# Channel statistics of an output projection: bn_stats on VectorE, or sums on ScalarE

## The chip, the cores and the metric

The kernel runs on one NeuronCore of one Trainium2 chip, in fp32 throughout. The metric is the device time of one execution in microseconds, the median of several runs. The engines are named as in the profile: PE (TensorE matmul; PEld is its weight load), DVE (VectorE), ACT (ScalarE), POOL (GpSimd), SP (SyncE, which issues nearly all DMAs).

## The reference, cut to what matters

Layer 0 is a Mamba-like block on x of shape (4, 128, 128, 128): batch B=4, C=128 channels, L=128*128=16384 positions, 256 inner channels, 16 states. Layer 1 is a group norm, a small softmax over four filters, and a product of 2D Fourier transforms.

```python
h1 = relu(xf @ mlp_w1.T + b1);  xm = h1 @ mlp_w2.T + b2
x_in, z = split(xm @ in_proj_w.T)
u = silu(causal_conv4(x_in) + conv_b)            # 256 channels
dt, Bm, Cm = split(u @ x_proj_w.T);  delta = softplus(dt @ dt_proj_w.T + dt_b)
h = h * exp(delta*A) + delta*u*Bm;  y = sum_s h*Cm   # a scan over L, 256 x 16 rows
y = (y + u*D) * silu(z)
out = y @ out_proj_w.T                            # C=128: the output projection
g = group_norm(out, 4 groups)                     # mean and variance over (C/4, H, W)
x1 = silu(g * gn_w + gn_b) + x
# layer 1: group norm of x1 (32 groups over x1 twice), 1x1 conv, relu, mean over (H, W),
# softmax over 4 filters; irfft2(sum_f w_f * X * FF_f) + residual_weight * x1
```

What the change touches is how the mean and variance of `out`, which the 4-group norm needs, are gathered.

## The kernel before, in words

`block0` (layer 0) cuts each batch into 32 chunks of T=512 positions, 128 chunks in all, and runs them as a software pipeline whose order is written out by hand: every piece of work is a Python function entered in `todo[slot, phase]`; a chunk has 16 slots (`NP`), and within a slot the phases run in the order turn, sums, pe, exps, late, act, pool, dbu, gate, scans, dve, end (L492 to L497). Each engine executes its own instructions in this order. Buffers come from pools, whose reuse adds waits.

**The scan.** A pair of slots is one unit of four scans (128 rows by 512 positions). `exps(n)` (L376) makes exp(delta*A) on ACT into four tiles `da0` to `da3`, of which three are single PSUM buffers; it stands one slot ahead of its use. `scans(n)` (L389) runs the recurrence on DVE (L405). In an even slot its two results go to a tile `h`, which POOL multiplies by C (L412). In an odd slot DVE multiplies them itself (L407), and ACT copies the last column out for the next chunk (L408, `st<-da`). `by_vector` (L338) decides which engine takes which h*C product. `dbu` (L344) makes delta*u*B on POOL (L354), and `sums` (L415) adds the states on PE (L426).

**The work beside it**, by its slot in the chunk: slot 2, `silu_act` (L227) for the chunk to come and `z_silu` (L232) on ACT, and `gate(1)` (L436) on DVE; slot 4, `o_mm` (L438), the output projection, and `xd_act` (L242); slot 5, `o_act` (L443), which copies the projection out of PSUM and sends it to a DRAM tile, and `dt_mm` (L255); slot 6, `dt_act` (L262), the softplus. Silu and softplus are in other activation tables than exp, so each brings an ACT_TABLE_LOAD before it and one before the next exp. `o_stats` (L451), the `bn_stats` of the projection, stands in slot 2 of the chunk after that one. (`o_mm` and `o_act` of a chunk lie in the slots of the next chunk, so that its statistics come two chunks late.)

The tag `pp` has two PSUM banks that are used in turn: convolution 0, convolution 1, (in some chunks two norm tiles), projection `po`, `dt` 0, `dt` 1. So `dt` 1 takes the bank that `po` leaves.

**Norming chunks.** While batch b+1 is scanned, batch b is finished (`finish`, L541): `group_norm` (L500) turns its statistics into mean and 1/std around slots 7 to 10 of one chunk; then in 16 chunks (`norming`, L329) two tiles each are normalised: `norm_act` (L563, Silu on ACT in slot 2), `norm_dve` (L568) and `norm_stats` (L573) on DVE in slot 3. There are 48 such chunks, and 80 plain ones, where DVE has no such work in slot 3. In the next 16 chunks `agg_act` (L598) runs Relu with an accumulator output on ACT. The last batch is finished inside `block1`, the Fourier part.

`which` is 0 for the 4-group norm of the projection and 1 for the norm of layer 1.

Of the kernel before, what the change touches and what calls it, by code (L numbers as in the profile page):

```python
# [26 lines left out]
F32 = mybir.dt.float32  # L27
AF = mybir.ActivationFunctionType
ALU = mybir.AluOpType
AX = mybir.AxisListType  # L30
# [3 lines left out]
P = 128  # L34
# [112 lines left out]
def block0(tc, s):  # L147
    nc, B, NCH, NH, NS, NG, ND, R, NX, KC, HALO, C, L, NF, DI = (
        s.nc, s.B, s.NCH, s.NH, s.NS, s.NG, s.ND, s.R, s.NX, s.KC, s.HALO, s.C, s.L, s.NF, s.DI,
    )  # L150
    NT = T // P
    with ExitStack() as ctx:
# [13 lines left out]
        def psum(n):  # L166
            return psp.tile([P, T], F32, tag="pp", name=f"pp_{n}")
# [5 lines left out]
        stats, outs = s.stats, s.outs  # L173
# [256 lines left out]
        def post(k):  # L430

            b, i = divmod(k, NCH)
            d = st[k]

            def gate(j):
                nc.vector.tensor_mul(d["zs"][:, j, :], d["zs"][:, j, :], d["y", j])  # L436

            def o_mm():  # L438
                d["po"] = psum(f"o_{k}")
                for j in range(NH):  # L440
                    nc.tensor.matmul(d["po"], s.wo[:, j, :], d["zs"][:, j, :], start=j == 0, stop=j == NH - 1)

            def o_act():  # L443
                if i == 0:
                    stats[b] = s.spool.tile([P, NCH, 6], F32, tag="stats", name=f"stats_{b}")
                    outs[b] = s.opool.tile([C, L], F32, tag="ob", name=f"ob_{b}")
                d["o"] = p2.tile([P, T], F32, tag="o", name=f"o_{k}", bufs=3)
                nc.scalar.copy(d["o"], d["po"])
                nc.sync.dma_start(out=outs[b][:, i * T : (i + 1) * T], in_=d["o"])

            def o_stats():  # L451
                nc.vector.bn_stats(stats[b][:, i, :], d["o"])
                st.pop(k - 1, None)

            return [
                (26, "dve", partial(gate, 0)), (34, "dve", partial(gate, 1)), (36, "pe", o_mm), (37, "act", o_act),
                (50, "dve", o_stats),
            ]

        n_chunks = B * NCH  # L460
# [1 line left out]
        for k in range(n_chunks):  # L462
            for at, phase, f in pre(k) + post(k):
                todo[at + (k - 1) * NP, phase].append(f)
# [35 lines left out]
def group_norm(s, io, b, mat, which, stat, at, then):  # L500


    nc = s.nc
    g = {}

    def small(n, m=1):
        g[n] = io.small.tile([P, m], F32, tag=n, name=f"{n}_{which}_{b}")
        return g[n]

    def aggregate():  # L510
        nc.vector.bn_aggr(small("mv", 2), stat().rearrange("p n q -> p (n q)"))

    def mean_mm():
        ps = g["ps"] = io.psum(f"gm_{which}_{b}")
        nc.tensor.matmul(ps[:, 0:1], getattr(s, mat), g["mv"][:, 0:1], start=True, stop=True)

    def spread_act():
        mv = g["mv"]
        nc.scalar.copy(small("mean"), g["ps"][:, 0:1])
        q = small("q")  # L520
        nc.scalar.activation(q, mv[:, 0:1], AF.Square, scale=-1.0, bias=g["mean"])
        nc.scalar.activation(q, q, AF.Identity, bias=mv[:, 1:2])

    def var_mm():
        ps = g["ps"] = io.psum(f"gv_{which}_{b}")
        nc.tensor.matmul(ps[:, 0:1], getattr(s, mat), g["q"], start=True, stop=True)

    def root_act():
        nc.scalar.activation(small("rstd"), g["ps"][:, 0:1], AF.Sqrt, bias=s.eps)

    def invert():
        nc.vector.reciprocal(g["rstd"], g["rstd"])
        then(g["mean"], g["rstd"])

    return [
        (at, "dve", aggregate), (at, "end", mean_mm), (at + 1, "act", spread_act), (at + 3, "pe", var_mm),
        (at + 3, "act", root_act), (at + 3, "dve", invert),
    ]
# [437 lines left out]
```

## Time and profile before

| | us |
|---|---|
| median of 3 runs (7328.43 to 7332.73) | 7330.66 |
| the profiled execution's own time | 7341.55 |
| its span | 7339.5 |
| block 0: last projection copy starts | 6525.7 |
| busy DVE / POOL / ACT / PE | 7022.4 / 6896.1 / 6064.9 / 5890.0 |
| `bn_stats` of the projection: 128 x 672 ns on DVE | 86.0 |
| its copy out of PSUM: 128 x 577 ns on ACT | 73.9 |

All durations come from the one profiled execution, whose time is 10.89 us (0.15%) above the median. A duration in the profile is longer than the distance to the next instruction's start on the same engine: neighbours overlap by some 0.09 us, so what an instruction takes from its engine is read from starts in the timeline.

### The profile page before, as it was taken

To read this page: it belongs to the slowest core of one execution; us is meant where nothing else is said; L and a number is where in the kernel's file an instruction comes from. 1 tells how busy PE (TensorE), PEld (TensorE's weight loads), DVE (VectorE), ACT (ScalarE), POOL (GpSimd) and SP (SyncE) were. 2 spreads that over 40 slices of the span, in tenths; PEclk is the share of its full clock that TensorE was granted. 3 is DMA by queue.
4 is the path that set the end of the run, shared out by engine and by line. 5 is a ranking of instruction groups with operands and counts; after the bars stand their busy time and mean duration, and the time that the engine had idled before them with its cause. 6 is when DMAs were issued, how large, how long until landed. Compare 5 with 4: busy or idle time off the path is not lost.

```text
span 7339.5 us, 90375 instructions
## 1 busy us (share of the span) xinstructions
PE 5890.0 (80%) x25908; PEld 2648.4 (36%) x25908; DVE 7022.4 (96%) x8168; ACT 6064.9 (83%) x13183; POOL 6896.1 (94%) x3188
## 2 busy tenths in 40 slices
PE   7877877877777788887777788887777788868999
PEld 2322322332222233332222233332222233348999
DVE  7999999999999999999999999999999999978777
ACT  6888888888888888888888888888888888867886
POOL 6999999999999999999999999999999999977787
PEclk8888888888888889898899888888999888889999
DMA  5766666666777767667777676677777766758666
GB/s 139 163 156 148 157 156 155 150 159 165 187 181 176 182 159 166 169 163 178 180 177 188 165 172 167 158 171 173 178 187 173 178 165 156 175 142 255 187 165 169
DMA packets 864134, 1246.32 MB, mean 170 GB/s; under 512 B 78856, under 2 KB 318608, under 8 KB 863632
## 3 DMA queue, kind: packets, MB, share of 16 engines
q1 hardware_dynamic: 863488, 1240.28, 69.2%
q8 instruction: 204, 3.34, 0.2%
q14 instruction: 298, 2.44, 0.1%
q10 hardware_dynamic: 144, 0.26, 0.0%
HBM read 996.97 MB, written 243.27 MB: 169 GB/s over the span
## 4 chain that ended last, share of the span: by engine, by line
DVE 16%; ACT 14%; DMA 14%; PE 12%; issue 5%; POOL 2%; SPq 1%; DVEq 0%; ACTq 0%; POOLq 0%
DVE da L405 7%; ACT da L387 6%; DVE h L405 4%; DMA rdelta<-dd 3%; DMA xt<-in_x 3%; DVE hb L407 2%; PE pp_h L190 2%; DMA of<-ob 2%; ACT bt L295 1%; DMA dd<-delta 1%; DMA rB<-bc 1%; PE pa L780 1%; DMA xr<-in_x 1%; ACT L387 1%; PE y L426 1%
## 5 line engine op out<-in xcount | busy, mean ns | idle before, releaser
L354 POOL TENSOR_TENSOR hb<-rdu,rB 128x1536 f32<-128x1536 f32 (+2 forms) x1536 | 3603.3, 2362 | 38.6 <-DMA rdu<-dd 35.3
L387 ACT ACTIVATE da<-rdelta,amat 128x512 f32<-128x512 f32 x4096 | 2677.1, 694 | 63.2 <-DVE h L405 60.0
L412 POOL TENSOR_TENSOR hb<-h,rC 128x1024 f32<-128x1024 f32 (+1 forms) x1072 | 2433.5, 2272 | 179.2 <-DVE h L405 162.5
L405 DVE TENSOR_TENSOR_SCAN da<-da,st,hb 128x512 f32<-128x512 f32 x1976 | 2425.0, 1272 | 11.7 <-POOL hb L354 5.3
L426 PE MATMUL y<-hb,sel 128*32 128x512 f32 x8192 | 1313.3, 717 | 3.1 <-POOL hb L412 2.7
L407 DVE TENSOR_TENSOR hb<-da,rC 128x512 f32<-128x512 f32 x2040 | 1301.3, 679 | 3.0
L405 DVE TENSOR_TENSOR_SCAN h<-da,st,b 128x512 f32<-128x512 f32 x992 | 1264.1, 1274 | 23.6 <-ACT da L387 7.0
L405 DVE TENSOR_TENSOR_SCAN h<-da,st,hb 128x512 f32<-128x512 f32 x1000 | 1256.8, 1261 | 2.0 <-ACT da L387 1.6
L374 PE MATMUL b<-ident,bt 128*128 128x128 f32 x4096 | 759.9, 309 | 613.3 <-DVE h L405 499.0
L225 PE MATMUL pp_cv<-xm,wck 128*128 128x512 f32 x2048 | 1018.7, 642 | 32.9 <-ACT zs L219 32.0
L374 PEld LDWEIGHTS b<-ident,bt 128*128 128x128 f32 x4096 | 548.7, 157 | 1187.2 <-DVE h L405 788.2
L295 ACT ACTIVATE bt<-pt_dut,xdt 128x256 f32<-128x256 f32 x2048 | 838.2, 471 | 132.4 <-PE pt_dut L284 132.3
L408 ACT COPY st<-da 128x1 f32<-128x1 f32 x2040 | 282.5, 161 | 767.9 <-DVE hb L407 765.8
L225 PEld LDWEIGHTS pp_cv<-xm,wck 128*128 128x128 f32 x2048 | 399.3, 206 | 700.2 <-issue 461.9
L190 PE MATMUL pp_h<-xt,w 128*128 128x512 f32 x512 | 387.3, 899 | 262.5 <-DMA xt<-in_x 208.3
L759 POOL TENSOR_TENSOR wb<-wb,term 128x1040 f32<-128x1040 f32 x192 | 461.0, 2401 | 90.0 <-ACT term L753 75.3
L284 PE MATMUL pt_dut<-ident,du 128*128 128x128 f32 x1024 | 209.3, 326 | 279.8 <-ACT st L408 270.3
L422 PE MATMUL y<-u,diag 128*128 128x512 f32 x512 | 297.8, 665 | 146.8 <-DVE zs L436 146.5
L303 POOL TENSOR_TENSOR du<-delta,u 128x512 f32<-128x512 f32 x256 | 319.1, 1268 | 27.2 <-ACT delta L266 27.2
L387 ACT ACT_TABLE_LOAD x262 | 336.1, 1283 | 4.7
L284 PEld LDWEIGHTS pt_dut<-ident,du 128*128 128x128 f32 x1024 | 126.9, 156 | 574.4 <-POOL du L303 436.2
L190 PEld LDWEIGHTS pp_h<-xt,w 128*128 128x128 f32 x512 | 124.6, 269 | 547.2 <-DMA xt<-in_x 261.1
(138 smaller groups left out, 8084.0 us busy)
## 6 DMA issues: line engine op xcount, KB each, us to landing
rdelta<-dd SPq DMA_DIRECT2D x1024, 256.0 KB, 4.8
rdu<-dd SPq DMA_DIRECT2D x1024, 256.0 KB, 7.8
rC<-bc SPq DMA_DIRECT2D x512, 256.0 KB, 7.5
rB<-bc SPq DMA_DIRECT2D x512, 192.0 KB, 4.8
dd<-delta SPq DMA_DIRECT2D x256, 256.0 KB, 7.3
dd<-du SPq DMA_DIRECT2D x256, 256.0 KB, 6.4
ft<-in_filt_w SPq DMA_DIRECT2D x104, 520.0 KB, 7.0
ob<-o SPq DMA_DIRECT2D x128, 256.0 KB, 2.1
```

The lines of the kernel that those rows point to most:

```text
L190: nc.tensor.matmul(ps["h", j], s.w1[:, j * P : (j + 1) * P], d["xt"], start=True, stop=True)
L225: nc.tensor.matmul(ps["cv", j], w, d["xm"][:, t : t + T], start=t == 0, stop=t == KC - 1)
L284: nc.tensor.transpose(ps["dut"][:, 2 * t + j, :], d["du"][:, j, at : at + P], s.ident)
L295: nc.scalar.activation(d["bt"][:, 2 * h + t, :, q, :], src, AF.Copy, scale=d["xdt"][:, 2 * h + t, R + q : R + q + 1])
L354: nc.gpsimd.tensor_tensor(hb[:, p : p + n, :], d["du", j][:, m : m + n, :], d["B"][:, p - 1 : p - 1 + n, :], ALU.mult)
L374: nc.tensor.transpose(b[:, t * P : (t + 1) * P], src, s.ident)
L387: nc.scalar.activation(d["da", p][q], d["delta", j][:, m, :], AF.Exp, scale=s.amat[:, c : c + 1])
L405: nc.vector.tensor_tensor_scan(o, das[q], b, init, ALU.mult, ALU.add)
L407: nc.vector.tensor_tensor(hb[:, p + q, :], das[q], d["C"][:, p + q, :], ALU.mult)
L412: nc.gpsimd.tensor_tensor(hb[:, ps, :], h[:, q, :], d["C"][:, ps, :], ALU.mult)
L426: nc.tensor.matmul(y[m * DG : (m + 1) * DG, :], s.sel, d["hb", j, r][:, p, :], start=False, stop=r == NG - 1)
L759: nc.gpsimd.tensor_tensor(wb, wb, u[n].terms[f], ALU.add)
```

## The change

The copy of the projection out of PSUM becomes an Identity activation with an accumulator output (the sum per channel), and a second activation, Square in place in PSUM with an accumulator output (the sum of squares), follows it. The `bn_stats` per chunk on DVE is gone; its place in the list only drops a dictionary entry. The statistics tile holds two rows of 32 sums per batch instead of 32 records of six. For this norm `bn_aggr` becomes a `reduce_sum`, and four small ACT instructions turn the sums into mean and variance ahead of the matmul that averages over the group. Which h*C products DVE and POOL take is as before, and so are all DMAs.

```diff
             def o_act():
                 if i == 0:
-                    stats[b] = s.spool.tile([P, NCH, 6], F32, tag="stats", name=f"stats_{b}")
+                    stats[b] = s.spool.tile([P, 2, NCH], F32, tag="stats", name=f"stats_{b}")
                     outs[b] = s.opool.tile([C, L], F32, tag="ob", name=f"ob_{b}")
                 d["o"] = p2.tile([P, T], F32, tag="o", name=f"o_{k}", bufs=3)
-                nc.scalar.copy(d["o"], d["po"])
+
+                nc.scalar.activation(d["o"], d["po"], AF.Identity, accum_out=stats[b][:, 0, i : i + 1])
+                nc.scalar.activation(d["po"], d["po"], AF.Square, accum_out=stats[b][:, 1, i : i + 1])
                 nc.sync.dma_start(out=outs[b][:, i * T : (i + 1) * T], in_=d["o"])
 
-            def o_stats():
-                nc.vector.bn_stats(stats[b][:, i, :], d["o"])
+            def done():
                 st.pop(k - 1, None)
 
             return [
...
-                (50, "dve", o_stats),
+                (50, "dve", done),
             ]
...
     def aggregate():
-        nc.vector.bn_aggr(small("mv", 2), stat().rearrange("p n q -> p (n q)"))
+        mv = small("mv", 2)
+        if which:
+            nc.vector.bn_aggr(mv, stat().rearrange("p n q -> p (n q)"))
+        else:
+            nc.vector.reduce_sum(mv, stat(), axis=AX.X)
 
     def mean_mm():
+        if which == 0:
+            mv, q = g["mv"], small("q")
+            nc.scalar.activation(q, mv[:, 0:1], AF.Square, scale=1.0 / s.L)
+            nc.scalar.mul(q, q, -1.0)
+            nc.scalar.mul(mv[:, 0:1], mv[:, 0:1], 1.0 / s.L)
+            nc.scalar.activation(mv[:, 1:2], mv[:, 1:2], AF.Identity, scale=1.0 / s.L, bias=q)
         ps = g["ps"] = io.psum(f"gm_{which}_{b}")
         nc.tensor.matmul(ps[:, 0:1], getattr(s, mat), g["mv"][:, 0:1], start=True, stop=True)
```

## The prediction

> **What bounds the kernel now.** The first row of the page gives two engines above 90% over the span.
>
> ```profile
> PE 5890.0 (80%) x25908; PEld 2648.4 (36%) x25908; DVE 7022.4 (96%) x8168; ACT 6064.9 (83%) x13183; POOL 6896.1 (94%) x3188
> ```
>
> In block 0 (the first 6560 us) the windows of 500 us show DVE at 489 to 498 us busy and POOL at 479 to 490. So DVE looks like the bound, and the edit takes work from it. The groups by form give that work, and the rows nearest to what is added (the copy that goes, L448, has 577 ns):
>
> ```profile
> L452 DVE BATCH_NORM_STATS2 stats<-o 128x6 f32<-128x512 f32 x128 | 86.0, 672 | 0.0
> L208 ACT ACTIVATE xm<-pp_xm,mlp_b 128x512 f32<-128x512 f32 x128 | 88.0, 687 | 3.5 <-PE pp_xm L200 3.5
> L600 ACT ACTIVATE pp_agg<-pp_agg,bv 128x512 f32<-128x512 f32 x84 | 54.0, 643 | 0.0
> L600 ACT ACTIVATION_READ_ACCUMULATOR pp_agg<-pp_agg,bv 128x1 f32 x84 | 16.1, 192 | 0.0
> ```
>
> A share of 99% doesn't say that DVE is what ends each wait. The timeline of a plain chunk does; first ACT, from slot 1's end to slot 6 (start, duration, both in us):
>
> ```profile
> 1310.81 0.16 ACT L408 COPY st<-da 128x1 f32<-128x1 f32 x1 [0.43 <-DVE hb L407]
> 1310.87 1.31 ACT L387 ACTIVATE da<-rdelta,amat 128x512 f32<-128x512 f32 x2
> 1312.19 1.28 ACT L233 ACT_TABLE_LOAD   x1
> 1313.49 1.06 ACT L233 ACTIVATE zs<-zs 128x1024 f32<-128x1024 f32 x1
> 1314.45 1.25 ACT L230 ACTIVATE u<-pp_cv,conv_b 128x512 f32<-128x512 f32 x2
> 1315.72 1.28 ACT L387 ACT_TABLE_LOAD   x1
> 1317.01 1.30 ACT L387 ACTIVATE da<-rdelta,amat 128x512 f32<-128x512 f32 x2
> ...
> 1321.55 0.58 ACT L448 COPY o<-pp_o 128x512 f32<-128x512 f32 x1
> 1323.20 0.16 ACT L408 COPY st<-da 128x1 f32<-128x1 f32 x1 [1.07 <-DVE hb L407]
> 1323.80 0.16 ACT L408 COPY st<-da 128x1 f32<-128x1 f32 x1 [0.43 <-DVE hb L407]
> ```
>
> and DVE over the same slots 2 to 4:
>
> ```profile
> 1313.06 0.67 DVE L452 BATCH_NORM_STATS2 stats<-o 128x6 f32<-128x512 f32 x1
> 1313.64 0.67 DVE L436 TENSOR_TENSOR zs<-zs,y 128x512 f32<-128x512 f32 x1
> ...
> 1317.78 1.27 DVE L405 TENSOR_TENSOR_SCAN h<-da,st,b 128x512 f32<-128x512 f32 x1
> ```
>
> ACT waits for DVE's last product of slot 1 (1310.81), then works without a gap through exps, a table load, three Silus, a second table load, and delivers the first exp for slot 4 at 1317.01 + 0.69 = 1317.70. DVE starts slot 4's scan at 1317.78, 0.044 us behind the modelled end of that exp. Where DVE does sit waiting for this exp (the first plain chunk of batches 1 to 3, where its scans are a little shorter), it starts 0.033 us behind it. So in slots 2 to 4 of a plain chunk **ACT and DVE are tied within 0.01 us**. Read at the same two places of the timeline, all plain chunks but those of the first batch's ramp show 0.03 to 0.05.
>
> The norming chunk is different. There DVE has four more instructions in slot 3, ACT only two more Silus (first ACT, then DVE):
>
> ```profile
> 1818.46 1.30 ACT L387 ACTIVATE da<-rdelta,amat 128x512 f32<-128x512 f32 x2
> ```
> ```profile
> 1817.86 1.28 DVE L570 TENSOR_TENSOR of<-pp_n,xr 128x512 f32<-128x512 f32 x2
> 1819.05 1.28 DVE L574 BATCH_NORM_STATS2 stats<-of 128x6 f32<-128x512 f32 x2
> 1820.24 1.27 DVE L405 TENSOR_TENSOR_SCAN h<-da,st,b 128x512 f32<-128x512 f32 x1
> ```
>
> The exp is ready at about 1819.15, DVE comes at 1820.24: 1.06 us behind, the same (1.05 to 1.06) in all 48 norming chunks. Here DVE alone is the bound.
>
> **What the Trainium skill says.** "ScalarE: Activation LUTs", section "What ACT_TABLE_LOAD costs", gives about 1283 ns for a load and 186 ns + 0.833 ns per element for an ACTIVATE with immediates, some 93 ns for each pointer operand, and neighbours that overlap by some 93 ns. The trace agrees: every load 1283, the copy 577 (613 by the page), Identity with a pointer bias 687 (706). "ScalarE activation tables: per-element evaluation and per-set limits", section "What a function is on this engine", says that two functions of one set need no load between them and that the accumulator output works with every table. In the trace neither Identity (L208) nor Square (L798, L799) has a load of its own, and the changed program's instruction list has 530 loads, as many as the program before. "SBUF — State Buffer", section "Who interferes with whom", says that a DVE instruction with at most one SBUF input outside the 2-port modes doesn't contend with GpSimd; if so, taking `bn_stats` away does not speed POOL up. No row before isolates that, and I count nothing for it.
>
> **The change part by part.**
>
> *bn_stats removed.* From start to start it takes 1313.64 − 1313.06 = 0.58, 0.586 on average; 128 of them are 75.0 us of DVE. In the 48 norming chunks it all counts: 1.06 − 0.586 leaves 0.47 of lead. POOL follows: its idle time in such a chunk is 1.05 us (0.89 of it before L412 in slot 4, waiting for DVE's h), so 0.47 remains there too. Gain 48 × 0.586 = **28.1 us**. In the 80 plain chunks the exp holds slot 4 where it is: gain 80 × 0.011 = 0.9 at most. What is late next there is ACT, by its two table loads, and DVE will stand 0.57 us before L405 in each.
>
> *o_act longer.* In the Relu rows with an accumulator output the read starts 0.57 us after the activation, and the next instruction 0.09 after the read (2902.53 to 2902.62). Identity to SBUF takes 0.58 to its successor (L208). The block is then 0.58 + 0.09 + 0.57 + 0.09 = 1.33 in place of 0.48: **0.85 us more**, 109 us of ACT in all. It lies in slot 5, where ACT waits 1.07 us for DVE's product and then 0.43 for the second one; only an excess over about 1.6 would delay the exps of slot 6. In a norming chunk the first wait is 1.65, less the 0.586 that DVE is earlier. Cost 0. If the cover went, each us would cost up to 128 us. Behind it stand the softplus and its two loads, after which DVE already waits 0.15 us in slot 8 of every chunk. The bounds: no overlap at all between the four instructions makes 0.69 + 0.19 + 0.66 + 0.19 = 1.73, an excess of 1.25, still 0; below nothing it can't go, since the copy waited for nobody.
>
> *The bank.* `dt` 1 waits for `po`'s bank until Square ends, about 1322.7 to 1323.0 instead of 1322.13. Its matmuls then end near 1324.0; the softplus reads at 1326.47 and PE's next work waits for DVE until 1325.0. Cost 0. SP's send of `o` starts 0.1 to 0.3 us later, and behind it stand loads of rB and rC, which wait for the landing of bc anyway. Cost 0.
>
> *Statistics.* Per batch, `bn_aggr` (1.01) becomes a sum (0.18 by L604). Four ACT instructions (0.23 to 0.33 apart by L521, L522 and L622, together 1.1 us) go in front of slot 8's exps, behind DVE's sum. ACT recovers 0.4 to 0.6 of it in its waits for DVE in slots 9 and 10; the rest delays the Sqrt for which DVE's reciprocal (L532) already waits 2.3 to 2.6 us. With the shorter sum: +0.3 (0 to 1.1) for each of 3 batches, **+0.9**. The last batch's matmul stands on the path in block 1: 0.85 less on DVE against 1.3 more on ACT, **+0.5**. At the end of block 0 the copy is followed by the softmax and then by block 1's first loads (last ACT instruction ends at 6527.35, first load at 6527.38): **+0.85**.
>
> Sum: −28.1 − 0.9 + 0.9 + 0.5 + 0.85 = **−26.8 us**. Against the profiled execution (7341.55, span 7339.5) that is 7314.8; the median of the runs stands 10.89 lower, so 7330.66 − 26.8 = **7303.9**.
>
> **The rivals.**
>
> A. *DVE is the bound everywhere*, and the whole 75.0 us counts, as the shares suggest: 7330.66 − 75.0 + 2.3 = 7258. Against it: the tie in all plain chunks. For it: only that the exps could move if ACT's chain began earlier, which no part of the edit does.
>
> B. *Nothing or a part is gained*, since POOL or a transfer holds the norming chunks. POOL's idle 1.05 us speaks against it; if half of it were needed for its own waits, the gain would be 48 × 0.3 = 14 us, 7319; with none, 7333.
>
> C. *Slower*: ACT's block in slot 5 outgrows its cover, and the exps of slots 6 and 7 and the softplus come late. It decides from an excess of 1.6 us; at 2.1 us, with accumulator reads that drain the engine, it costs 128 × 0.5 = 64, so 7330.66 + 64 − 27 = 7368. Against it: the Relu rows show no such drain.
>
> D. *It doesn't do what it says*: a load of another table around each Square would cost 128 × (2 × 1.28 + 0.85 − 1.6) = 232 us. The count of loads excludes it.
>
> **How the numbers follow.** A measurement can tell about 0.2% from no change, 14.7 us. Main case 0.78 (7296 to 7312), A 0.05, B 0.11, C 0.06, D nil. Main and A are faster by over 0.2%, with a little of B: 0.83; B gives within 0.2%: 0.1; C slower: 0.07. The range takes in the main case, the best part of B and a gain a little past the main case: 7290 to 7321.
>
> **What would show it.** Right: 128 bn_stats gone; plain chunks of the same length (49.2 and 49.95 us in turn between the `xd` copies) with 0.57 us of idle DVE before L405 in slot 4, released by ACT's exp; norming chunks at 50.55 instead of 51.13; POOL's wait in slot 4 of those down from 0.9 to 0.3; Identity and Square with two reads 1.33 us apart from start to next. Wrong: plain chunks that shrink (A), a wait of the slot 6 or slot 8 scans for exps that grows above 0.15 (C), or norming chunks that stay at 51.1 (B).

## The result and the profile after

| | before | after |
|---|---|---|
| median, us (8 runs each) | 7338.79 (7328.43 to 7344.72) | 7315.54 (7304.67 to 7319.75) |
| the profiled execution | 7341.55 | 7313.21 |
| ratio of the times, 95% interval | | 0.9969 (0.9961 to 0.9978) |

The changed kernel is faster by 22.8 us by the ratio (16 to 29 by its interval); between the two profiled executions it is 28.3, against the forecast 26.8. With more runs the median before came out 8 us higher than the three runs that the forecast was set against, so its 7303.9 is best read as a ratio, 0.9964. In absolute terms the median of 7315.54 is 11.6 above the forecast; 8.1 of these are the higher median before.

The first row of the page after. DVE has lost 72.9 us of busy time and ACT has gained 83.8:

```profile
PE 5969.1 (82%) x25908; PEld 2667.5 (36%) x25908; DVE 6949.5 (95%) x8040; ACT 6148.7 (84%) x13583; POOL 6895.5 (94%) x3188
```

The groups by form of the new block (count, busy us, mean ns, idle time before). Each of the two activations has a row of its own for the read of its accumulator, and none has a table load:

```profile
L449 ACT ACTIVATE o<-pp_o 128x512 f32<-128x512 f32 x128 | 75.3, 588 | 2.5 <-PE pp_o L441 2.5
L450 ACT ACTIVATE pp_o<-pp_o 128x512 f32<-128x512 f32 x128 | 74.3, 581 | 0.0
L449 ACT ACTIVATION_READ_ACCUMULATOR o<-pp_o 128x1 f32 x128 | 24.6, 192 | 0.0
L450 ACT ACTIVATION_READ_ACCUMULATOR pp_o<-pp_o 128x1 f32 x128 | 24.0, 187 | 0.0
```

The timeline of the same plain chunk as before, ACT from the end of slot 1 to slot 6 (start, duration, both in us):

```profile
1306.97 0.16 ACT L408 COPY st<-da 128x1 f32<-128x1 f32 x1 [0.43 <-DVE hb L407]
...
1308.35 1.28 ACT L233 ACT_TABLE_LOAD   x1
1309.64 1.06 ACT L233 ACTIVATE zs<-zs 128x1024 f32<-128x1024 f32 x1
1310.60 1.25 ACT L230 ACTIVATE u<-pp_cv,conv_b 128x512 f32<-128x512 f32 x2
1311.87 1.28 ACT L387 ACT_TABLE_LOAD   x1
1313.16 1.30 ACT L387 ACTIVATE da<-rdelta,amat 128x512 f32<-128x512 f32 x2
...
1317.70 0.59 ACT L449 ACTIVATE o<-pp_o 128x512 f32<-128x512 f32 x1
1318.19 0.19 ACT L449 ACTIVATION_READ_ACCUMULATOR o<-pp_o 128x1 f32 x1
1318.28 0.58 ACT L450 ACTIVATE pp_o<-pp_o 128x512 f32<-128x512 f32 x1
1318.80 0.19 ACT L450 ACTIVATION_READ_ACCUMULATOR pp_o<-pp_o 128x1 f32 x1
1319.35 0.16 ACT L408 COPY st<-da 128x1 f32<-128x1 f32 x1 [0.36 <-DVE hb L407]
```

and DVE in slots 2 to 4:

```profile
1309.22 0.65 DVE L436 TENSOR_TENSOR zs<-zs,y 128x512 f32<-128x512 f32 x1
1309.80 2.45 DVE L405 TENSOR_TENSOR_SCAN da<-da,st,hb 128x512 f32<-128x512 f32 x2
1312.17 1.26 DVE L407 TENSOR_TENSOR hb<-da,rC 128x512 f32<-128x512 f32 x2
1313.92 1.28 DVE L405 TENSOR_TENSOR_SCAN h<-da,st,b 128x512 f32<-128x512 f32 x1 [0.49 <-ACT da L387]
```

From the last copy of slot 1 (1306.97) to the first exp for slot 4 (1313.16) ACT needs 6.19 us; before it needed 6.20. The scan of slot 4 starts 0.033 us behind the end of that exp (the median of all plain chunks), which is the distance that the prediction took for a scan that waits. What was `bn_stats` is now a wait. Two products and their overlap would bring DVE to that scan at 1312.17 + 1.19 = 1313.36; it starts at 1313.92, 0.56 later (the bracket shows 0.49, since neighbours usually overlap). The table of waits says the same for the whole run (total us, times, longest): first before, then after. The longest, some 40 us, is the wait at the start of the kernel; without it 25 waits of 11.5 us together have become 98 of 51.6.

```profile
DVE h L405 <- ACT da L387: 52.8, 26, 41.3
```
```profile
DVE h L405 <- ACT da L387: 91.7, 99, 40.1
```

In a norming chunk after (ACT, then DVE, then POOL) the first exp ends at 1815.87 + 0.69 = 1816.56 and DVE arrives at 1817.07, without a wait and 0.51 behind it where it had been 1.09. POOL still waits 0.30 us for DVE in slot 4, where it had waited 0.89; its line before stands last:

```profile
1815.87 1.30 ACT L387 ACTIVATE da<-rdelta,amat 128x512 f32<-128x512 f32 x2
```
```profile
1814.68 1.28 DVE L581 TENSOR_TENSOR of<-pp_n,xr 128x512 f32<-128x512 f32 x2
1815.87 1.27 DVE L585 BATCH_NORM_STATS2 stats<-of 128x6 f32<-128x512 f32 x2
1817.07 1.26 DVE L405 TENSOR_TENSOR_SCAN h<-da,st,b 128x512 f32<-128x512 f32 x1
```
```profile
1819.58 2.35 POOL L412 TENSOR_TENSOR hb<-h,rC 128x1024 f32<-128x1024 f32 x1 [0.30 <-DVE h L405]
```
```profile
1822.77 2.34 POOL L412 TENSOR_TENSOR hb<-h,rC 128x1024 f32<-128x1024 f32 x1 [0.89 <-DVE h L405]
```

**Chunk lengths.** The distance between the `xd` copies of successive chunks, read from the timeline, makes a budget of block 0. It runs from slot 4 of one chunk to slot 4 of the next. A plain length is called even or odd by the first of the two, and a norming length holds the norming work of slot 3 of the second. The table gives, for the before kernel, the changed one and each experiment, the median length of even plain, odd plain and norming chunks, away from the ends of a batch (35, 33 and 45 of them), and "irregular": by how much the sum of these 113 lengths exceeds what it would be with each at the median of its kind.

| kernel | even plain | odd plain | norming | irregular, us | ratio to before (95%) |
|---|---|---|---|---|---|
| before | 49.21 | 49.95 | 51.13 | 17.7 | 1 |
| after | 49.19 | 49.94 | 50.53 | 21.2 | 0.9969 (0.9961 to 0.9978) |
| e1_plain_only | 49.20 | 49.95 | 51.13 | 24.6 | 0.9999 (0.9991 to 1.0007) |
| e2_norming_only | 49.21 | 49.95 | 50.54 | 27.4 | 0.9968 (0.9955 to 0.9981) |
| e3_sums_beside | 49.21 | 49.95 | 51.13 | 21.0 | 1.0003 (0.9995 to 1.0011) |
| e5_before_no_zsilu | 49.20 | 49.95 | 51.13 | 12.6 | 0.9981 (0.9974 to 0.9987) |
| e4_after_no_zsilu | 48.69 | 49.45 | 50.54 | 15.6 | 0.9918 (0.9904 to 0.9931) |
| e7_before_moved | 49.39 | 49.77 | 51.13 | 15.3 | 0.9993 (0.9984 to 1.0001) |
| e6_after_moved | 49.25 | 49.32 | 50.54 | 28.1 | 0.9948 (0.9936 to 0.9961) |
| e8_after_moved_even | 48.92 | 49.36 | 50.54 | 19.1 | 0.9929 (0.9917 to 0.9942) |
| e11_before_load | 49.20 | 49.95 | 51.13 | 3.7 | 0.9972 (0.9962 to 0.9982) |
| e12_before_no_zsilu_load | 49.20 | 49.95 | 51.13 | 1.6 | 0.9964 (0.995 to 0.9978) |
| e9_after_load | 49.20 | 49.94 | 50.54 | 3.7 | 0.9934 (0.9921 to 0.9946) |
| e10_even_load | 48.91 | 49.36 | 50.54 | 2.1 | 0.9876 (0.9863 to 0.989) |

Between the two profiled executions: 45 norming chunks gain 45 × 0.60 = 27.0, and 5.8 comes back as more irregularity in them; plain chunks gain 3.5, of which 2.3 is irregularity; the 12 chunks around the batch ends gain 4.3 (three of these are norming: 1.8); the start gains 1.9; and what follows the last chunk takes 2.7 more. That is 28.

### The profile page after: what moved, and what is told of

Its sections match the earlier page's. It is cut to its first block, busy times and chain, and to the rows that moved or that the text cites. A ratio compares the mean times of both kernels' runs of the same rounds, so it can differ in the third digit from the quotient of the medians.

```text
span 7311.3 us, 90639 instructions
## 1 busy us (share of the span) xinstructions
PE 5969.1 (82%) x25908; PEld 2667.5 (36%) x25908; DVE 6949.5 (95%) x8040; ACT 6148.7 (84%) x13583; POOL 6895.5 (94%) x3188
## 4 chain that ended last, share of the span: by engine, by line
DMA 16%; ACT 16%; DVE 12%; PE 12%; issue 5%; POOL 2%; SPq 1%; DVEq 0%; ACTq 0%; POOLq 0%
ACT da L387 6%; DVE da L405 6%; DMA xt<-in_x 3%; DMA rdelta<-dd 3%; DVE h L405 3%; DMA dd<-delta 2%; DVE hb L407 2%; DMA rB<-bc 2%; DMA of<-ob 2%; PE pp_h L190 2%; ACT L387 1%; DMA xr<-in_x 1%; ACT bt L295 1%; PE y L426 1%; PE pa L791 1%
## 5 line engine op out<-in xcount | busy, mean ns | idle before, releaser
L426 PE MATMUL y<-hb,sel 128*32 128x512 f32 x8192 | 1331.8, 726 | 4.8 <-POOL hb L412 2.9
L258 PE MATMUL pp_dt<-xd,wdt 8*128 8x512 f32 x512 | 290.1, 649 | 80.1 <-ACT pp_o L450 79.2
```

The source lines that it names most:

```text
L426: nc.tensor.matmul(y[m * DG : (m + 1) * DG, :], s.sel, d["hb", j, r][:, p, :], start=False, stop=r == NG - 1)
```

## The experiments

The theory: in plain chunks ACT's chain of table loads and Silus sets slot 4, tied with DVE, so `bn_stats` counts in norming chunks alone; the longer ACT block lies in a wait. The rivals: A, DVE is the bound in every chunk; B, POOL holds the norming chunks; C, ACT's block outgrows its cover.

### bn_stats left out in one kind of chunk only: e1 and e2

Both are the kernel before with a condition in front of `bn_stats`, and the statistics tile filled once per batch.

```diff
# e1_plain_only
-                nc.vector.bn_stats(stats[b][:, i, :], d["o"])
+                if norming(k + 2):
+                    nc.vector.bn_stats(stats[b][:, i, :], d["o"])
# e2_norming_only
-                nc.vector.bn_stats(stats[b][:, i, :], d["o"])
+                if not norming(k + 2):
+                    nc.vector.bn_stats(stats[b][:, i, :], d["o"])
```

> The kernel before, with bn_stats left out in the 80 chunks where its place is a plain chunk, and kept in the 48 norming ones (the statistics are then partly a constant). Tie theory (ACT's two table loads hold slot 4 of a plain chunk): 0 to -2 us; plain chunks stay 49.2 and 49.95 us long and DVE stands 0.49 us idle before L405 in slot 4. Rival A (DVE is the bound everywhere): 80 x 0.586 = -47 us, plain chunks 48.6 and 49.4.

> The mirror: bn_stats left out only where its place is a norming chunk (48), kept in the 80 plain ones. Tie theory: the whole gain, 48 x 0.586 = -28 us, norming chunks 50.54 instead of 51.13. Rival B (POOL holds the norming chunks): -14 us or less. Rival A gives -28 here too, so that this run tells A from the tie only beside its mirror.

Measured beside 7345.09 us for the kernel before: e1 7344.95 (ratio 0.9999, 0.9991 to 1.0007), e2 7318.99 (0.9968, 0.9955 to 0.9981). Eighty `bn_stats` off the busiest engine gained nothing that can be told from zero; the other 48 gained 23.5 us by the ratio, as much as the whole change (22.8). DVE's timeline in e1 shows where the time of a plain chunk goes:

```profile
1313.18 1.27 DVE L407 TENSOR_TENSOR hb<-da,rC 128x512 f32<-128x512 f32 x2
1314.95 1.28 DVE L405 TENSOR_TENSOR_SCAN h<-da,st,b 128x512 f32<-128x512 f32 x1 [0.50 <-ACT da L387]
```

The same wait as in the changed kernel, with nothing changed on ACT: so it is ACT's old chain, tied with DVE, that holds the plain chunks, and not the new ACT work. A falls, and B falls by e2's 50.54.

### The ACT block alone: e3

```diff
-                nc.scalar.copy(d["o"], d["po"])
+                nc.scalar.activation(d["o"], d["po"], AF.Identity, accum_out=sums2[b][:, 0, i : i + 1])
+                nc.scalar.activation(d["po"], d["po"], AF.Square, accum_out=sums2[b][:, 1, i : i + 1])
```

> The kernel before, bn_stats kept and used, with the copy made into Identity and Square with sums that nobody reads (a second small tile): the added ACT work alone, 0.72 us a chunk by the profile after. Tie theory: it lies in ACT's wait of slot 5, 0 to +2 us (only the end of block 0). Rival C (ACT's length counts): up to 128 x 0.72 = +92 us, with exps of slots 6 to 8 late.

Measured: 7345.49 us, 1.0003 (0.9995 to 1.0011). ACT's timeline, at the end of the block:

```profile
1318.82 0.58 ACT L451 ACTIVATE pp_o<-pp_o 128x512 f32<-128x512 f32 x1
1319.34 0.19 ACT L451 ACTIVATION_READ_ACCUMULATOR pp_o<-pp_o 128x1 f32 x1
1319.90 0.16 ACT L409 COPY st<-da 128x1 f32<-128x1 f32 x1 [0.37 <-DVE hb L408]
```

ACT still waits 0.37 us for DVE's product after the block, where it waited 1.07 before it was lengthened. The difference, 0.70, is the block's growth, and all of it comes out of the wait. C falls.

### ACT's chain shortened: e5 and e4

If ACT's chain ties with DVE, shortening it must do nothing for the kernel before and open the wait in the changed one. The Silu of z (1.06 us) is left out.

```diff
-                (NP - 3, "pe", z_mm), (NP - 1, "act", z_act), (NP + 2, "act", z_silu), (3, "pe", xd_mm), ...
+                (NP - 3, "pe", z_mm), (NP - 1, "act", z_act), (3, "pe", xd_mm), ...
```

> The kernel before with z_silu left out (z goes into the gate without its Silu): ACT's work between the two table loads of slot 2 is 0.96 us shorter, with bn_stats still on DVE. Tie theory: DVE alone then holds slot 4, plain chunks stay at 49.2 and 49.95, 0 to -4 us. If ACT rather than DVE were what holds these chunks: up to 80 x 0.57 = -46 us.

> The changed kernel with z_silu left out (z goes into the gate without its Silu): ACT's chain of slot 2 is 0.96 us shorter than the 0.57 us that bn_stats had. Tie theory: the gap before L405 in slot 4 closes and the 80 plain chunks gain what they did not: 80 x 0.57 = -46 us on the changed kernel, -69 us on the kernel before (ratio about 0.9906), plain chunks 48.6 and 49.35. Rivals (POOL or transfers hold the plain chunks): it stays at -23 us.

Measured: e5 (from before) 7329.87, 0.9981 (0.9974 to 0.9987), 14 us faster than before; e4 (from the changed kernel) 7275.73, 0.9918 (0.9904 to 0.9931), 60 us faster than the kernel before (69 expected) and so some 37 faster than the changed one (46 expected). In e4 slot 4 begins without a wait in an undisturbed plain chunk:

```profile
1313.83 1.27 DVE L407 TENSOR_TENSOR hb<-da,rC 128x512 f32<-128x512 f32 x2
1315.01 1.27 DVE L405 TENSOR_TENSOR_SCAN h<-da,st,b 128x512 f32<-128x512 f32 x1
```

The commonest lengths in e4's timeline are 48.61 us for even and 49.36 for odd plain chunks, 0.58 less than in the changed kernel and as expected: `bn_stats` is worth its full 0.586 in a plain chunk once ACT gets out of the way. The medians of the table, 48.69 and 49.45, lie higher because only a third of e4's plain lengths are undisturbed. Counted from 48.61 and 49.36 the irregular part of e4's plain lengths is 18 us, where the changed kernel has 14. By the profiled spans e4 gains 40 us on the changed kernel.

In e5 the plain chunks kept their 49.20 and 49.95, as the tie says. But the 14 us were a miss: more than the 0 to 4 expected, and not in any regular chunk. Of the 7.8 us between the two profiled spans, 5.1 are irregular length and 5.2 lie around the batch ends, with 2.5 lost elsewhere. So the irregular chunks had to be looked at, which led to the last group.

### DVE's work moved ahead of the wait: e7, e6, e8

The new idle time in slot 4 can be used if h\*C work that DVE does behind it is moved ahead of it. In an odd plain chunk DVE takes one extra product in slot 12; here it takes the one in slot 2. In e8 even plain chunks also swap: DVE takes the product in slot 2 and gives one of slot 13 to POOL.

```diff
# e7_before_moved (on before) and e6_after_moved (on after)
-            return p > 1 or (k % 2 == 1 and (j, r, p) == (1, 2, 1))
+            return p > 1 or (k % 2 == 1 and (j, r, p) == (0, 1, 1))
# e8_after_moved_even (on after)
-            return p > 1 or (k % 2 == 1 and (j, r, p) == (1, 2, 1))
+            if k % 2 == 0:
+                return (p > 1 and (j, r, p) != (1, 2, 2)) or (j, r, p) == (0, 1, 1)
+            return p > 1 or (j, r, p) == (0, 1, 1)
```

> The same one-line move in the kernel before, where slot 2 still has bn_stats and no hole. Tie theory: DVE's work is the same and only stands elsewhere, so 0 (-4 to +4 us). If the move were good in itself: about -24 us.

> The changed kernel with one line more: in odd plain chunks DVE takes its extra h*C product in slot 2 (unit 1) instead of slot 12 (unit 6); shares unchanged, all results kept. Tie theory: the product fills the hole of slot 2, odd plain chunks go from 49.94 to about 49.3: 40 x 0.6 = -24 us on the changed kernel (-18 to -30), about -47 us on the kernel before. If DVE's total held the chunks: 0 on the changed kernel. If ACT's chain grows by the copy out of slot 2 (0.08 to 0.16): up to 6 us less gain.

> As the move above, and in even plain chunks too: DVE takes a product in slot 2 and gives one of slot 13 (unit 6) to POOL, results kept. Tie theory: even plain chunks from 49.19 to about 48.7, where POOL's 48.5 us of work comes into sight: -20 us beyond the move alone, about -44 us on the changed kernel. If POOL binds as soon as it is touched: no gain beyond the move, or a few us lost.

Measured beside 7339.49 for before: e7 7334.52, 0.9993 (0.9984 to 1.0001); e6 7296.93, 0.9948 (0.9936 to 0.9961); e8 7288.96, 0.9929 (0.9917 to 0.9942). The same edit shifts 0.18 us from odd to even chunks in the kernel before, with no effect clear of the noise. In the changed one it takes 0.62 off the odd length and adds only 0.06 to the even one: the product leaves an odd length, and slot 2 of an odd chunk lies in the even length before it, at whose end DVE had waited. The idle time was real, and only the changed kernel has it.

Yet by the ratios e6 gains some 15 us on the changed kernel and e8 some 29, by the profiled spans 17 and 42, where 24 and 44 were expected. For e6 the table shows why: its odd chunks fell as expected, but its irregular part is 7 us larger than in the changed kernel. Even chunks in e8 fell to 48.92, not 48.7. In e8's odd lengths POOL waits for nobody any more; in its even ones POOL waits 1.6 us for DVE and DVE stands idle for 0.2, so there DVE still sets the pace. Where the missing 0.2 us of the even chunk went was not traced.

### The load of x issued earlier: e11, e12, e9, e10

First the mechanism, in the kernel before. An irregular chunk on ACT, and the scan of slot 12 in it on DVE:

```profile
1288.86 0.69 ACT L195 ACTIVATE h<-pp_h,mlp_b 128x512 f32<-128x512 f32 x1 [1.52 <-issue]
1290.52 0.69 ACT L195 ACTIVATE h<-pp_h,mlp_b 128x512 f32<-128x512 f32 x1 [0.97 <-PE pp_h L190]
1291.10 1.29 ACT L387 ACTIVATE da<-rdelta,amat 128x512 f32<-128x512 f32 x2
```
```profile
1291.85 1.28 DVE L405 TENSOR_TENSOR_SCAN h<-da,st,b 128x512 f32<-128x512 f32 x1 [0.53 <-ACT da L387]
```

The exps stand behind L195 in ACT's order, L195 waits for PE's `pp_h`, and PE waits for the load of x:

```profile
1286.69 3.78 PE L190 MATMUL pp_h<-xt,w 128*128 128x512 f32 x4 [3.00 <-DMA xt<-in_x]
```

That load had been issued some 9 us earlier, on SP, right behind the two transfers of delta, which wait for the softplus:

```profile
1276.20 0.92 SPq L268 DMA_DIRECT2D dd<-delta  x2
1277.43 0.51 SPq L185 DMA_DIRECT2D xt<-in_x  x1
```

The experiment issues it one slot earlier. e11 is before with this edit, e12 is e11 without the Silu of z, e9 is the changed kernel with it, and e10 is e8 with it.

```diff
-                (-9, "pe", load), (-7, "pe", h1_mm), (-6, "act", h1_act), ...
+                (-10, "pe", load), (-7, "pe", h1_mm), (-6, "act", h1_act), ...
```

> The earlier load alone on the kernel before. Late-load theory: -13 us (its trace has 18 us of excess), regular chunks unchanged at 49.2, 49.95 and 51.13. Rival: 0.

> The kernel before without the Silu of z (z goes into the gate unchanged), with the earlier load. If the 14 us that leaving z_silu out gave were fewer late loads, they are not there a second time: 0 to -5 us against the earlier load alone. If they came from ACT's shorter chain: -14 us against it again.

> The changed kernel with the load of xt entered one slot earlier (10 slots ahead in place of 9), so that SP issues it ahead of the two dd writes that wait for the softplus. Theory of late loads (chunks of odd length come from ACT's h1 waiting for xt): the 21 us by which such chunks exceed the regular length in the trace of the changed kernel go down to 5 or less, regular lengths stay: -15 us on the changed kernel (-8 to -22), about -38 us on the kernel before. Rival (the odd chunks come from the transfers of dd and rdu): 0, or slower, since dd now stands behind xt.

> The same earlier load on the version with the moved products in odd and even plain chunks. If the two add up: a further -15 us, about -65 us on the kernel before (ratio 0.991). If POOL, which is idle for 0.0 us in odd chunks there, takes the late loads up already: no gain.

Measured beside 7343.75 for before: e11 7322.25, 0.9972 (0.9962 to 0.9982); e12 7316.52, 0.9964 (0.995 to 0.9978); e9 7294.86, 0.9934 (0.9921 to 0.9946); e10 7252.71, 0.9876 (0.9863 to 0.989). In e9 SP now issues the load ahead of delta:

```profile
1320.61 0.36 SPq L185 DMA_DIRECT2D xt<-in_x  x1
1321.56 1.16 SPq L268 DMA_DIRECT2D dd<-delta  x2
```

A slot is some 3 us, but the load gains less, since the transfers of rC are still issued before it: counted from the last `xd` copy it is issued at 7.1 us in place of 8.9 (medians of e9 and the changed kernel; 7.3 in place of 9.4 in e11 and before), and PE's first matmul on it starts 0.8 to 1.0 us earlier. PE's wait for the load falls to about a half, and ACT's wait behind it to a third; first the changed kernel, then e9 (total us, times, longest):

```profile
PE pp_h L190 <- DMA xt<-in_x: 257.9, 121, 8.6
...
ACT h L195 <- PE pp_h L190: 54.9, 73, 7.6
```
```profile
PE pp_h L190 <- DMA xt<-in_x: 139.5, 90, 8.5
...
ACT h L195 <- PE pp_h L190: 17.6, 22, 7.6
```

The irregular part falls from 17.7 to 3.7 us on before and from 21.2 to 3.7 on after; by the ratio e9 gains 26 us over the changed kernel, by the two profiles 18.6. All four gained more than expected, e9 by the ratio; by its profile it lies inside what was expected. The scatter shrinks too: the five runs of e9 lie within 4.1 us, the four of e10 within 3.5, where the eight of the changed kernel spread over 15; the eight of e11 lie within 10, the twelve of the kernel before beside them within 21.

On the miss of e5: with the loads early, leaving z's Silu out moves the profiled span from 7320.2 to 7320.0, and the medians by 6 us with intervals that overlap. That fits the theory that most of e5's 14 us had to do with late loads, to which a shorter chain on ACT may leave more room. How that comes about is not shown, and what the last 6 us are stays open: the runs themselves overlap (7320.59 to 7330.55 with the Silu, 7315.81 to 7323.38 without).

**e10 beats both kernels**: 7252.71 us, 91 below the kernel before on the same chip. It has the sums on ScalarE, the moved products and the earlier load. From e8 to e10 the medians, of two chips, fall by 36 us and the profiled spans only by 15 (7269.3 to 7254.1): e8's profiled execution was the fastest of its runs, which spread over 22 us.

## Why the prediction was right

- *The split of the 75 us.* Right, in place and size. Norming chunks 50.53 where 50.55 was forecast; plain chunks 49.19 and 49.94, unchanged, with 0.56 us of idle time before slot 4's scan where 0.57 was forecast, released by ACT's exp. e1 and e2 show both halves separately, e4 and e6 show that the idle time is one that can be had back. The tie was real: a plain chunk got 0.017 us shorter where the forecast had 0.011. This lead of a hundredth of a microsecond, read from the starts in the timeline, decided between a gain of 27 and one of 75.
- *POOL.* Right: its wait in slot 4 of norming chunks fell from 0.89 to 0.30, and it held nothing back. Its busy time stayed the same (6896.1 and 6895.5 us), as the sum had assumed.
- *The ACT block.* Its cost of nothing was right (e3), its length not: 1.33 us was forecast and 1.20 came (0.49 + 0.09 + 0.52 between starts, and 0.10 for the last read), so 0.72 more than before and not 0.85. The terms that were too big are the two activations. They were taken from L208 and L600, which have 687 and 643 ns; Identity and Square here have 588 and 581. The wait behind the block shrank from 1.07 to 0.36, so 0.36 us of cover is left, not the 0.2 that 1.33 would have left.
- *The bank.* `dt`'s matmuls do wait for Square now, 79.2 us in all for PE (L258 waiting for L450), and e3 shows that this costs nothing.
- *Statistics and ends.* +0.9, +0.5 and +0.85 were forecast. The chunks around the batch ends took 2.5 us less beside their three norming chunks, so the first cost isn't to be seen. What follows the last chunk took 2.7 more against 1.35, but that part varies between 902.5 and 908.3 us among the kernels that have it as it was before. These terms stay unresolved. Between the two profiles, all that isn't a regular chunk adds up to a cost of 1.8 (3.5 more irregular length and 2.7 at the end, less 2.5 around the batch ends and 1.9 at the start), close to the 2.25 of the forecast. That closeness is luck, since none of these parts was forecast at its size, and so the agreement of 28.3 with 26.8 is in part luck too.
- *What was missing.* The sum had no term for late loads: 17.7 us of irregular length before, 21.2 after. The runs scatter less once the load is early, so this part probably differs from one execution to the next, and the difference of medians (22.8 by the ratio) and that of two profiles (28.3) need not agree; the interval covers both. The kernel before has late loads too. The growth lies in the norming chunks alone, where the irregular part rose from 1.2 to 7.0 us; in plain chunks it fell from 16.5 to 14.2. Among the kernels without the earlier load, those without `bn_stats` in norming chunks have 2.7 to 9.0 us there, those with it 1.2 to 3.7; with the earlier load all have 0.1 or less. This would fit a loss of cover: in a norming chunk the scan of slot 12, which the late exps of the example feed, starts 2.12 us behind its exp before and 1.76 after. No experiment tests that link.

## What to carry to other kernels

When the busiest engine is relieved, ask in each stage how late the second engine is: the distance between the scan's start and the end of the exp it consumes was 0.04 us in one kind of chunk and 1.1 in the other, and that told which `bn_stats` were worth anything. A median over chunks can mislead here: in the kernel without the Silu of z it hid that undisturbed chunks had gained all of the 0.58. A wait that opens where work was taken away is room: moving other work of the same engine ahead of it (a product from slot 12 to slot 2) turned it into time, while the same move in the kernel before was worth nothing clear of the noise. And when a part of the gain shows up in no regular chunk, look for a transfer that lands late in some of them and stands in front of in-order work.

## What the runs showed of the hardware

An accumulator output on ScalarE costs a row of 187 to 192 ns after its activation, but half of it overlaps: from its start to the next instruction's start is 0.09 us (1318.19 to 1318.28). Identity from PSUM to SBUF with the accumulator was 588 ns against 577 for the plain copy, and Square in place in PSUM 581, so two passes over 128x512 with both sums take 1.20 us of ACT where `bn_stats` took 0.586 of DVE. The unexpected part was the queue: whether SP issued a load of 256 KB ahead of two transfers that wait for the softplus or behind them, about 2 us of difference in the time of its issue, was worth 21 us (13 to 28) on the kernel before.
